# A graph network's layer 0: flags at its end, fewer small vector operations, ranks as whole rows

## The chip, the cores and the metric

The kernel runs on one core of one Trainium2 chip. A core has five engines that run their own instruction streams: TensorE (PE; the loading of its weights is shown apart as PEld), VectorE (DVE), ScalarE (ACT), GpSimd (POOL) and SyncE (SP), which here only issues transfers. Sixteen DMA engines move data between HBM and the core's memory. The metric is the time of one execution on the device in microseconds; a version's time is the median of its runs.

## The reference

Four graph layers work on 2708 nodes with 512 features. Each adds its result to x, and works on h, the normalised and clipped x. The change lies in layer 0, and in the flags that its rows set.

```python
def _L0_gnn_ref(cur, incidence_m):
    mask = incidence_m > 0
    head = mask.astype(...)
    head = head / max(sqrt(sum(head * head, axis=-1)), 1e-12)
    inc = incidence_m + head
    return inc @ cur / sum(inc, axis=-1)
...
h = maximum(_layernorm(x), 0);  x = x + _L0_gnn_ref(h, adj)
h = maximum(_layernorm(x), 0);  x = x + _L1_gnn_ref(h, adj, Wks, Wqs, Wvs, Wo)
h = maximum(_layernorm(x), 0);  x = x + _L2_gnn_ref(h, adj, W1, b1, W3, b3, Wf, bf)
h = maximum(_layernorm(x), 0);  x = x + _L3_gnn_ref(h, adj, W, b)
```

Layer 1 is attention with eight heads, where a score is masked by 1e16 x (1 - adj). With such a factor the softmax of a row is 1 at the row's greatest entry and 0 elsewhere, so the kernel only needs the place of that entry. This holds if no second entry ties with it, if no entry is negative, and if the scores are bounded. The kernel sets a flag where one of these fails, and then runs a general path after the fast one.

## The kernel before, in words

The adjacency is mostly zeros, and its nonzeros lie densest in the first columns and rows. The nodes are cut into NT = 22 tiles of 128 rows (the last has 20). Of a tile m's row of the adjacency, the first DENSE = 6 column tiles are used whole. Of the rest, only the columns that are nonzero somewhere in the tile are fetched, in CHUNKS[m] groups of 128 columns (10 down to 2). The first three tiles use all columns.

Layer 0 is one loop over the tiles (L782), with work for later tiles mixed in:

- *Statistics of a tile* (stats_to, L690). A slab of 128 adjacency rows is loaded (L498). ScalarE takes signs and their sum (L524), clips them and counts (L529), and takes the root of the count (L530). VectorE holds it above 1e-12 (L531) and inverts it (L532): that is rn, the 1/norm. flag_negative (L500) compares the sum of the signs with the count. The row sum is taken (L543) and 1/degree worked out. attended (L549) finds the eight greatest entries of each row (L556) and their places (L558), copies the first place to idx (L559), and scores the first two against each other (L560, L563). Each flag goes into its own column of bad.
- *Lists of columns.* Three tiles form a group. TensorE adds their signs over the rows (count, L265), in four blocks of 485 columns that stand below each other on the partitions. rank_blocks (L316) clips these counts to 0 and 1 (L322) and scans them (L328), so that each column has its rank, and writes the ranks to DRAM (L329) as 128 rows of 485. For each tile load_ranks (L354) reads its four pieces back, spread over all 128 partitions (L362). search (L371) writes an end mark behind the last rank (L378, L379), and finds for each place 1, 2, 3... the first column of that rank (L385). The found column becomes an index for the rows of h (L386), and, in two operations (L395, L403), an index for the adjacency. A last operation (L406) compares the end mark with the capacity of the list.
- *Gathers.* gather_adj (L569) and gather_rows (L588) fetch the listed pieces of the adjacency and rows of h, one indirect transfer from POOL's queue for each 128 places.
- *The incidence* (L626). The 1/norm of a tile's 128 rows is wanted along the free axis, on all partitions. VectorE scales an identity by rn (L631), and TensorE multiplies a matrix of ones with it (L633). Two operations per piece then make mask times 1/norm and add the adjacency (L636, L644), in pieces inc (whole tiles) and incl (listed columns).
- *The product* (L794) adds inc and incl times h in PSUM. Then x is updated (L807), normalised again, and multiplied with the values' weights for layer 1 (after, L727).

What an engine does next is a fixed order. The program is written as above, and a scheduling framework orders each engine's stream when the kernel is built, from its own estimate of what things cost; it also sets the waits between engines. A change in the number of operations can therefore change the order of others. Transfers issued by SP go through one queue in order, and an SP instruction that waits holds back all behind it. Loads of slabs (L498), of dense pieces (L618), of ranks (L362) and of x (L746), and stores of counts (L286), ranks (L329), lists (L659), y (L740) and x1 (L750) all stand in that queue. POOL's queue holds the gathers. Slabs have three buffers, ranks two, gathered pieces three, and gathered rows of h sixteen slots.

After the loop the degrees are added up (L290), and layer 1 gathers rows of y by idx (L1067). The flags are added up in layer 1 and looked at when layer 3 is done (L1371).

Of the kernel before, what the change touches and what calls it, by code (L numbers as in the profile page):

```python
# [9 lines left out]
FP = mybir.dt.float32  # L10
FR = mybir.dt.float32r
BF = mybir.dt.bfloat16
HF = mybir.dt.float16
# [29 lines left out]
def kernel(  # L43
# [89 lines left out]
    rank_b = dram.tile([NGROUP, P, WIDE], HF, name="rank_b")  # L133
    rank_l = dram.tile([1, N], HF, name="rank_l")

    idx = const.tile([P, NT], U32, name="idx")
    BAD_BOUND, BAD_NEG, BAD_MANY = NT, NT + 1, 2 * NT + 1
# [88 lines left out]
    with tc.tile_pool(name="l0_slab", bufs=2) as slabs, tc.tile_pool(  # L226
# [17 lines left out]

        counts = hp.tile([P, GROUP, QUAD], BF, name="counts")
# [70 lines left out]
        def rank_blocks(ms, last_block):  # L316

            rk = hp.tile([P, WIDE], HF, name="rk")  # L320
            sums, offs = (wp.tile([P, 1], FP, name=name) for name in ("sums", "offs"))
            nc.vector.tensor_scalar(  # L322
                rk, last_block, 1.0, None, op0=ALU.min, op1=ALU.add, accum_out=sums
            )
            ahead = ps_list.tile([P, BLK], FP, name="list")
            nc.tensor.matmul(ahead[:, :1], ahead_of, sums, start=True, stop=True)
            nc.scalar.copy(offs, ahead[:, :1])
            nc.vector.tensor_tensor_scan(rk, rk, rk, offs[:, 0:1], ALU.add, ALU.max)  # L328
            nc.sync.dma_start(out=rank_b[ms[0] // GROUP], in_=rk)  # L329

        def rank_rows(ms):

            both = in_slab()
            m = ms[-1]
            r = m % GROUP + 1
            first = dense_of(m) * P
            total = both[QUAD : QUAD + r, :N].bitcast(BF)
            rank = both[:r, :N]
            load_counts(m // GROUP, r, total)
            nc.vector.tensor_scalar_min(rank[:, first:], total[:, first:], 1.0)  # L340
            nc.vector.tensor_tensor_scan(
                rank[:, first:], rank[:, first:], rank[:, first:], 0.0, ALU.add, ALU.max
            )
            if first:
                nc.sync.dma_start(
                    out=rank_b[m // GROUP].rearrange("(b i) w -> i b w", b=4)[:r],
                    in_=rank[:, first:].rearrange("i (b w) -> i b w", b=4),
                )
            else:
                nc.sync.dma_start(out=rank_l, in_=rank)  # L350
# [3 lines left out]
        def load_ranks(m):  # L354
            first = dense_of(m) * P
            num = N - first
            if first:
                ranks = slabs.tile([P, N + 1 - BEHIND], HF, name="ranks", bufs=2)
                q = m % GROUP

                row = rank_b[m // GROUP].rearrange("(b i) w -> i b w", b=4)[q : q + 1]
                nc.sync.dma_start(  # L362
                    out=ranks[:, :num].rearrange("p (b w) -> p b w", b=4),
                    in_=row.to_broadcast([P, 4, WIDE]),
                )
            else:
                ranks = in_slab()[:, : N + 1]
                nc.sync.dma_start(out=ranks[:, :N], in_=rank_l.to_broadcast([P, N]))
            ranks_of[m] = ranks

        def search(m):  # L371
# [5 lines left out]
            end = wp.tile([P, 1], FP, name="end")  # L377
            nc.vector.tensor_scalar_add(end, ranks[:, num - 1 : num], 1.0)  # L378
            nc.vector.tensor_copy(ranks[:, num : num + 1], end)  # L379
            want = wp.tile([P, NCH], FP, name="want")  # L380
            nc.vector.tensor_scalar(want, places, end, None, op0=ALU.min)
            for c0 in range(0, CHUNKS[m], 8):
                c = slice(c0, c0 + 8)
                at = wp.tile([P, 8], U32, name="found")
                nc.vector.max_index(at, want[:, c], ranks)  # L385
                nc.vector.tensor_scalar(  # L386
                    idx_g[:, m, c],
                    at,
                    float(N - first),
                    float(first),  # L390
                    op0=ALU.min,
                    op1=ALU.add,
                )
                node = wp.tile([P, 8], FP, name="node")
                nc.vector.tensor_scalar(  # L395
                    node,
                    at,
                    float(N - 1 - first),
                    float(N // UNIT),
                    op0=ALU.min,  # L400
                    op1=ALU.mult,
                )
                nc.vector.tensor_scalar_add(  # L403
                    idx_a[:, m, c], node, float((first * N + m * P) // UNIT)
                )
            nc.vector.tensor_scalar(  # L406
                bad[:, BAD_MANY + m : BAD_MANY + m + 1],
                end,
                float(CHUNKS[m] * P + 1),
                None,  # L410
                op0=ALU.is_gt,
            )

# [86 lines left out]
        def flag_negative(m, sum_sgn, cnt):  # L500
            n = rows(m)
            nc.vector.tensor_tensor(
                bad[:n, BAD_NEG + m : BAD_NEG + m + 1], sum_sgn[:n], cnt[:n], ALU.not_equal
            )

        def count_signs(m, last):

            sgn = slabs.tile([P, N], BF, name="sgn", bufs=GROUP)
            cnt, sum_sgn = (wp.tile([P, 1], FP, name=name, bufs=4) for name in ("cnt", "sum_sgn"))
            behind(sgn[:1, :1], last)  # L510
            nc.scalar.activation(sgn, slab[m], AF.Sign, accum_out=sum_sgn)
            nc.scalar.activation(sgn, sgn, AF.Relu, accum_out=cnt)
            flag_negative(m, sum_sgn, cnt)

        def row_norm(m):
# [5 lines left out]
            cnt, sum_sgn = (wp.tile([P, 1], FP, name=name, bufs=4) for name in ("cnt", "sum_sgn"))  # L521
# [3 lines left out]
            if m in LATE:  # L525
                cnt = sum_sgn
# [3 lines left out]
            nc.scalar.activation(rn[:n], cnt[:n], AF.Sqrt)  # L530
            nc.vector.tensor_scalar_max(rn[:n], rn[:n], NORM_EPS)  # L531
            nc.vector.reciprocal(rn[:n], rn[:n])  # L532
            if m not in LATE:
                flag_negative(m, sum_sgn, cnt)
# [14 lines left out]
        def attended(m):  # L549
# [5 lines left out]
            top = wp.tile([P, 8], FP, name="top")  # L555
            nc.vector.max(top[:n], ar[:n])  # L556
            at_top = wp.tile([P, 8], U32, name="at_top")
            nc.vector.max_index(at_top[:n], top[:n], ar[:n])  # L558
            nc.vector.tensor_copy(idx[:n, m : m + 1], at_top[:n, 0:1])  # L559
            nc.vector.tensor_scalar(  # L560
                top[:n, 0:2], top[:n, 0:2], 1.0, MASK_SCALE, op0=ALU.subtract, op1=ALU.mult
            )
            nc.vector.tensor_tensor(  # L563
                bad[:n, m : m + 1], top[:n, 1:2], top[:n, 0:1], ALU.is_ge
            )
# [3 lines left out]
        def gather_adj(m):  # L569

            n, num = rows(m), CHUNKS[m]
            for c0 in range(0, num, NCL):
                k = min(NCL, num - c0)
                ac = slabs.tile([P, NCL, P], FP, name="ac", bufs=3)
                for c in range(k):
# [3 lines left out]
                        in_=adj_units,  # L579
                        in_offset=bass.IndirectOffsetOnAxis(  # L580
# [45 lines left out]
        def incidence(m):  # L626
# [3 lines left out]
            dg = wp.tile([P, P], FP, name="dg")  # L630
            nc.vector.tensor_scalar(dg[:n, :n], ident[:n, :n], rn[:n], None, op0=ALU.mult)  # L631
            rb = ps_small.tile([P, P], FP, name="rb")
            nc.tensor.matmul(rb[:, :n], ones[:n], dg[:n, :n], start=True, stop=True)  # L633
# [207 lines left out]
        flush()  # L841
        degrees()
# [3 lines left out]
        flush()  # L846

# [951 lines left out]
```

## Time and profile before

| what | value |
|---|---|
| median of 3 runs | 1415.01 us (1413.84 to 1416.62) |
| profiled execution | 1402.04 us, of which the span is 1400.2 us |
| PE busy | 1278.4 us (91%) |
| DVE busy | 946.6 us (68%) |
| ACT busy | 687.1 us (49%) |
| POOL busy | 662.7 us (47%) |
| mean granted TensorE clock | 0.964 |
| layer 0 | 0 to about 460 us |
| first product of layer 1 (L902) | 477.0 us |

The span reaches from the first to the last instruction of the profiled execution. Busy times are those of instructions that overlap on one engine counted once; a row's mean duration is that of one instruction from its own start to its own end, so the durations of neighbours may overlap. Waits are put down to what came last before the instruction could start. "L531" is a line of the kernel before. Transfers are not counted as work of an engine; the DMA share is how far the sixteen DMA engines were busy.

### The profile page before, as it was taken

The numbers are of one execution on the slowest core, as the hardware profiler recorded it, in microseconds if no ns is written. First come the engines' busy times: TensorE is split into PE (matmuls) and PEld (weight loads), VectorE is DVE, ScalarE is ACT, GpSimd is POOL, SyncE is SP. The second block draws the span as 40 slices with busy tenths as digits, with TensorE's granted clock in tenths as the row PEclk, the third lists the DMA queues.
The fourth block names the chain that finished last, engine by engine and source line by source line (L and its number), as shares of the span: only waits on it lengthen the run. The fifth ranks groups of instructions, "written<-read, shape, count | busy, mean of one in ns | idle before, by whom it ended". The sixth has DMA issues, their size and how long they took to land.

```text
span 1400.2 us, 15615 instructions
## 1 busy us (share of the span) xinstructions
PE 1278.4 (91%) x4478; PEld 768.7 (55%) x4478; DVE 946.6 (68%) x1944; ACT 687.1 (49%) x1051; POOL 662.7 (47%) x673
## 2 busy tenths in 40 slices
PE   4889798998997489899999999899999999978997
PEld 2334344443443357555656666466666666656876
DVE  4778999897997687533434446365666666668686
ACT  5885756742445465422333335244455544556553
POOL 1256677766754411265444441333334344635762
PEclk9999999999998799999999999999999999989999
DMA  9999899999993785487777777756555665858984
GB/s 344 361 306 324 285 379 349 337 331 274 323 323 119 265 295 177 144 269 253 249 214 237 242 222 225 256 166 192 170 165 177 196 203 189 246 160 282 299 262 161
DMA packets 196872, 349.04 MB, mean 249 GB/s; under 512 B 22198, under 2 KB 109840, under 8 KB 193045
## 3 DMA queue, kind: packets, MB, share of 16 engines
q1 hardware_dynamic: 149177, 200.80, 43.0%
q0 software_dynamic: 46032, 145.05, 32.4%
q10 hardware_dynamic: 1568, 2.10, 0.4%
q8 instruction: 37, 0.61, 0.2%
q14 instruction: 58, 0.48, 0.1%
HBM read 284.58 MB, written 63.29 MB: 248 GB/s over the span
## 4 chain that ended last, share of the span: by engine, by line
PE 54%; DMA 5%; DVE 2%; ACT 1%; issue 1%; SPq 0%; POOL 0%; DVEq 0%; ACTq 0%; POOLq 0%
PE aggs L1014 15%; PE main L927 10%; PE agg L1011 8%; PE mixed L927 5%; PE aggs L1011 4%; PE pt L902 3%; PE agg L1202 2%; PE aggs L1202 2%; PE aggs L1026 2%; DMA nz<-nz 1%; DMA wb<-hid 1%; PE pt L1202 1%; PE agg L927 1%; DMA gg<-g1d,idx_g 1%; DMA raw<-in_adj_t_dram 1%
## 5 line engine op out<-in xcount | busy, mean ns | idle before, releaser
L1014 PE MATMUL aggs<-gg,ac 128*128 128x512 f32 (+1 forms) x520 | 233.0, 596 | 3.6 <-DMA gg<-g1d,idx_g 3.6
L962 POOL DMA_INDIRECT gg<-g2d,idx_g x130 | 131.0, 1008 | 218.4 <-PE aggs L1014 170.2
L962 POOL DMA_INDIRECT gg<-g1d,idx_g x130 | 133.6, 1027 | 173.4 <-PE aggs L1014 103.3
L576 POOL DMA_INDIRECT ac<-in_adj_t_dram,idx_a x130 | 133.6, 1028 | 89.3 <-issue 31.3
L794 PE MATMUL acc<-h,inc 128*128 128x512 f32 (+1 forms) x348 | 163.2, 617 | 12.8 <-DVE inc L644 12.6
L1014 PEld LDWEIGHTS aggs<-gg,ac 128*128 128x128 f32 (+1 forms) x520 | 97.9, 189 | 110.7 <-issue 102.4
L594 POOL DMA_INDIRECT h<-h0d,idx_g x111 | 113.3, 1021 | 33.8 <-issue 21.3
L998 ACT ACTIVATE a_hi<-raw 128x384 fp32r<-128x384 f32 x84 | 43.6, 520 | 160.7 <-issue 87.2
L1011 PE MATMUL agg<-ghi,a_hi 128*128 128x512 f32 x252 | 114.9, 456 | 3.3 <-ACT a_hi L998 3.1
L794 PEld LDWEIGHTS acc<-h,inc 128*128 128x128 f32 (+1 forms) x348 | 65.4, 196 | 91.6 <-issue 74.0
L1011 PE MATMUL agg<-glo,a_lo 128*128 128x512 f32 x252 | 102.1, 405 | 3.2 <-ACT glo L207 3.2
L794 PE MATMUL acc<-h,incl 128*128 128x512 f32 (+1 forms) x222 | 103.3, 611 | 0.0
L1011 PE MATMUL aggs<-gs,a_s 128*128 128x512 f32 x252 | 100.5, 402 | 0.6 <-DVE gs L204 0.6
L999 DVE TENSOR_TENSOR a_lo<-raw,a_hi 128x384 fp32r<-128x384 f32 x84 | 47.2, 562 | 73.5 <-ACT a_hi L998 45.2
L158 PE MATMUL yacc<-wvo,hT 128*128 128x512 f32 (+1 forms) x176 | 85.6, 627 | 3.2 <-ACT hT L193 3.2
L908 DVE SCALAR_TENSOR_TENSOR v_lo<-pt,v_hi 128x512 fp32r<-128x512 f32 (+1 forms) x88 | 56.4, 664 | 44.6 <-ACT v_hi L907 44.1
L962 POOL DMA_INDIRECT gg<-hidr,idx_h x62 | 64.8, 1046 | 42.7 <-PE aggs L1202 16.4
L889 DVE SCALAR_TENSOR_TENSOR u<-aggs,u 128x512 f32<-128x512 f32 x42 | 28.8, 686 | 76.6 <-PE aggs L1014 75.1
L907 ACT ACTIVATE v_hi<-pt 128x512 fp32r<-128x512 f32 (+1 forms) x88 | 48.4, 578 | 45.0 <-PE pt L902 43.1
L794 PEld LDWEIGHTS acc<-h,incl 128*128 128x128 f32 (+1 forms) x222 | 42.5, 196 | 50.4 <-issue 47.8
L524 ACT ACTIVATE sgn<-ar 128x2708 bf16<-128x2708 f32 (+1 forms) x22 | 54.0, 2455 | 27.1 <-DMA ar<-in_adj_dram 26.6
L556 DVE MAX8 top<-ar 128x8 f32<-128x2708 f32 (+1 forms) x22 | 65.3, 2969 | 0.0
(321 smaller groups left out, 2788.9 us busy)
## 6 DMA issues: line engine op xcount, KB each, us to landing
ar<-in_adj_dram SPq DMA_DIRECT2D x27, 1354.0 KB
raw<-in_adj_t_dram SPq DMA_DIRECT2D x122, 192.0 KB
slot<-x SPq DMA_DIRECT2D x41, 256.0 KB
at<-in_adj_t_dram SPq DMA_DIRECT2D x27, 384.0 KB
ranks<-rank_b SPq DMA_DIRECT2D x20, 485.0 KB
ac<-lst SPq DMA_DIRECT2D x16, 384.0 KB
h<-in_x_dram SPq DMA_DIRECT2D x21, 256.0 KB
h0d<-h POOLq DMA_DIRECT2D x21, 256.0 KB, 7.2
```

The source lines that it names most:

```text
L158: nc.tensor.matmul(acc[:n], hT[:, c, :n], w[:, c, :], start=(c == 0), stop=(c == NCD - 1))
L524: nc.scalar.activation(sgn[:n], ar[:n], AF.Sign, accum_out=sum_sgn[:n])
L556: nc.vector.max(top[:n], ar[:n])
L576: nc.gpsimd.indirect_dma_start(out=ac[:, c, :n], out_offset=None, in_=adj_units, in_offset=bass.IndirectOffsetOnAxis(ap=idx_a[:, m, c0 + c ...
L594: nc.gpsimd.indirect_dma_start(out=g, out_offset=None, in_=h0d[:, :], in_offset=bass.IndirectOffsetOnAxis(ap=idx_g[:, m, c : c + 1], axis=0),)
L794: product = nc.tensor.matmul(acc[:n], a, g, start=(i == 0), stop=(i == len(pairs) - 1))
L908: nc.vector.scalar_tensor_tensor(lo[d], pt[d], 0.0, hi[d].bitcast(FP), op0=ALU.max, op1=ALU.subtract)
L927: nc.tensor.matmul(acc[:n], a[:, c, :n], b[:, c, :], start=first and c == 0, stop=last and c == NCD - 1,)
L962: nc.gpsimd.indirect_dma_start(out=gs[c], out_offset=None, in_=gd[:, :], in_offset=bass.IndirectOffsetOnAxis(ap=index[:, m, c : c + 1], ax ...
L1011: nc.tensor.matmul(acc[:n], a[:k, i, :n], b[:k], start=st, stop=sp)
L1014: nc.tensor.matmul(mixed[:n], a, g, start=(c == 0 and not dense_of(m)), stop=(c == len(chunks) - 1),)
L1202: nc.tensor.matmul(bank_h(m)[: rows(m)], a, b, start=(i == 1), stop=(i == total))
```

## The change

Five things change, all in layer 0.

- The greatest entries (tops, at_top), the counts and sign sums (cnts, sums_sgn) and the end marks (ends) of all tiles are kept in tiles with one column per row tile. A new function flags() works all flags out from these, once, after the loop. Flags move to other columns of bad. idx is copied once for all tiles.
- The lower bound of the norm goes into the root as a bias of 1e-24, so the maximum falls away. Its place in the order is ScalarE's L539, then the inverse.
- 1/norm is spread by one product of rn, read 128 times along the free axis, with the identity. The scaled identity is gone.
- A search makes the adjacency's index in one operation. The constant part of the address is given to the indirect transfer as an offset.
- Ranks are stored with their end mark as whole rows of 1941 elements. rank_blocks adds 1 behind the last rank and writes its four blocks with four transfers; rank_rows adds it likewise. load_ranks reads one contiguous row, spread over the partitions, and search only copies the end mark.

```diff
-    rank_b = dram.tile([NGROUP, P, WIDE], HF, name="rank_b")
-    rank_l = dram.tile([1, N], HF, name="rank_l")
+    rank_b = dram.tile([NGROUP, GROUP, 4 * WIDE + 1], HF, name="rank_b")
+    rank_l = dram.tile([1, N + 1], HF, name="rank_l")
...
+        for t, v in ((cnts, 0.0), (sums_sgn, 0.0), (ends, 0.0), (tiny, NORM_EPS * NORM_EPS)):
+            nc.gpsimd.memset(t, v)
+        for t in range(NT):
+            nc.gpsimd.memset(caps[:, t : t + 1], float(CHUNKS[t] * P + 1))
...
+        def flags():
+
+            score = wp.tile([P, NT, 2], FP, name="score", bufs=1)
+            nc.vector.tensor_scalar(
+                score, tops[:, :, 0:2], 1.0, MASK_SCALE, op0=ALU.subtract, op1=ALU.mult
+            )
+            nc.vector.tensor_tensor(bad[:, :NT], score[:, :, 1], score[:, :, 0], ALU.is_ge)
+            nc.vector.tensor_tensor(
+                bad[:, BAD_NEG : BAD_NEG + NT], sums_sgn, cnts, ALU.not_equal
+            )
+            nc.vector.tensor_tensor(bad[:, BAD_MANY : BAD_MANY + NT], ends, caps, ALU.is_gt)
...
-            nc.sync.dma_start(out=rank_b[ms[0] // GROUP], in_=rk)
+            nc.vector.tensor_scalar_add(end, row_end[:, wide - 1 : wide], 1.0)
+            for b in range(4):
+                w = wide + b // 3
+                nc.sync.dma_start(
+                    out=rank_b[ms[0] // GROUP, : len(ms), b * wide : b * wide + w],
+                    in_=row_end[b * QUAD : b * QUAD + len(ms), :w],
+                )
...
-                nc.sync.dma_start(
-                    out=ranks[:, :num].rearrange("p (b w) -> p b w", b=4),
-                    in_=row.to_broadcast([P, 4, WIDE]),
-                )
+                row = rank_b[m // GROUP, q : q + 1, : num + 1]
...
+            nc.sync.dma_start(out=ranks, in_=row.to_broadcast([P, num + 1]))
...
-            end = wp.tile([P, 1], FP, name="end")
-            nc.vector.tensor_scalar_add(end, ranks[:, num - 1 : num], 1.0)
-            nc.vector.tensor_copy(ranks[:, num : num + 1], end)
+            end = ends[:, m : m + 1]
+            nc.vector.tensor_copy(end, ranks[:, num : num + 1])
...
-                node = wp.tile([P, 8], FP, name="node")
                 nc.vector.tensor_scalar(
-                    node,
+                    idx_a[:, m, c],
                     at,
                     float(N - 1 - first),
                     float(N // UNIT),
                     op0=ALU.min,
                     op1=ALU.mult,
                 )
-                nc.vector.tensor_scalar_add(
-                    idx_a[:, m, c], node, float((first * N + m * P) // UNIT)
-                )
-            nc.vector.tensor_scalar(
-                bad[:, BAD_MANY + m : BAD_MANY + m + 1],
-                end,
-                float(CHUNKS[m] * P + 1),
-                None,
-                op0=ALU.is_gt,
-            )
...
-            nc.scalar.activation(rn[:n], cnt[:n], AF.Sqrt)
-            nc.vector.tensor_scalar_max(rn[:n], rn[:n], NORM_EPS)
+            nc.scalar.activation(rn[:n], cnt[:n], AF.Sqrt, bias=tiny[:n])
             nc.vector.reciprocal(rn[:n], rn[:n])
-            if m not in LATE:
-                flag_negative(m, sum_sgn, cnt)
...
-            nc.vector.tensor_copy(idx[:n, m : m + 1], at_top[:n, 0:1])
-            nc.vector.tensor_scalar(
-                top[:n, 0:2], top[:n, 0:2], 1.0, MASK_SCALE, op0=ALU.subtract, op1=ALU.mult
-            )
-            nc.vector.tensor_tensor(
-                bad[:n, m : m + 1], top[:n, 1:2], top[:n, 0:1], ALU.is_ge
-            )
...
+                        element_offset=dense_of(m) * P * N + m * P,
...
-            dg = wp.tile([P, P], FP, name="dg")
-            nc.vector.tensor_scalar(dg[:n, :n], ident[:n, :n], rn[:n], None, op0=ALU.mult)
             rb = ps_small.tile([P, P], FP, name="rb")
-            nc.tensor.matmul(rb[:, :n], ones[:n], dg[:n, :n], start=True, stop=True)
+            nc.tensor.matmul(
+                rb[:, :n], rn[:n].to_broadcast([n, P]), ident[:n, :n], start=True, stop=True
+            )
...
         flush()
+        nc.vector.tensor_copy(idx, at_top[:, :, 0])
         degrees()
...
         flush()
+        flags()
```

## The prediction

> **What bounds the kernel now.** The page comes first: which engines are busy in the slices that layer 0 fills (a slice is 35 us, so the first 13).
>
> ```profile
> PE   4889798998997489899999999899999999978997
> DVE  4778999897997687533434446365666666668686
> POOL 1256677766754411265444441333334344635762
> DMA  9999899999993785487777777756555665858984
> ```
>
> PE, DVE and the DMA engines all stand at 8 or 9. So I cut out the stretch in which the vector engine has no rest, from 80 us (the first list is searched) to 452 us (the last row maximum), and the part of it in which the gathers run densest:
>
> ```profile
> 80.00:452.00 372.00, 336.38 (x913) 151.11 (x912) 346.09 (x723) 206.38 (x251) 248.47 (x244) 0.96 0.90 304
> 80.00:290.00 210.00, 193.58 (x542) 87.03 (x541) 196.27 (x428) 137.67 (x161) 147.16 (x150) 0.97 0.94 325
> ```
>
> The columns are length, then busy us (and instructions) of PE, PEld, DVE, ACT, POOL, then clock, DMA share, GB/s. Of 372 us DVE works 346, PE 336. What is left is told by the waits of the first 500 us:
>
> ```profile
> DVE end L378 <- DMA ranks<-rank_b: 21.0, 6, 6.3
> PE acc L794 <- DVE inc L644: 12.6, 7, 3.4
> PE rb L633 <- DVE dg L631: 9.6, 6, 3.7
> PE rb L633 <- DVE deg L544: 3.8, 1, 3.8
> ```
>
> DVE hardly waits for anything but rank lists; PE's idle time ends at DVE. DVE is therefore the engine that sets the pace, PE is 10 us of work behind it, and a stall of DVE goes straight to PE. One such place, from the timelines of DVE and PE:
>
> ```profile
> 224.88 0.15 DVE L378 TENSOR_SCALAR end<-ranks 128x1 f32<-128x1 f16 x1 [3.26 <-DMA ranks<-rank_b]
> 224.95 0.17 DVE L178 BATCH_NORM_AGGREGATE mv<-stats 128x2 f32<-128x6 f32 x1
> 225.04 0.12 DVE L531 TENSOR_SCALAR rn<-rn 128x1 f32<-128x1 f32 x1
> 225.08 0.15 DVE L379 CAST ranks<-end 128x1 f16<-128x1 f32 x1
> ...
> 228.62 0.27 DVE L631 TENSOR_SCALAR dg<-ident,rn 128x128 f32<-128x128 f32 x1
> 228.80 2.98 DVE L556 MAX8 top<-ar 128x8 f32<-128x2708 f32 x1
> ```
> ```profile
> 220.02 5.32 PE L794 MATMUL acc<-h,inc 128*128 128x512 f32 x12
> 229.03 0.77 PE L633 MATMUL rb<-dg,ones 128*128 128x128 f32 x2 [3.69 <-DVE dg L631]
> 229.59 7.69 PE L794 MATMUL acc<-h,incl 128*128 128x512 f32 x12
> ```
>
> A late rank list (3.26 us) makes the scaled identity late, and PE stands still for 3.69. After it twelve rows take 7.69 us where twelve took 5.32 before: the granted clock was 0.88 and 0.78 in the slices 220 to 240. A gap of PE so costs about 2.4 us more than its length.
>
> **The change, part by part.**
>
> *DVE instructions taken away.* Six kinds go once per row tile, 22 each: the max on the norm (L531), the scaled identity (L631), the copy of the index (L559), the score and its comparison (L560, L563), the sign comparison (L502): 132. Of a search go the bound flag (L406) and one of the two that make the end mark (L378, L379), 21 each, and of 23 groups of places one of two (L395, L403). That is 132 + 42 + 23 = 197.
>
> What one costs is the choice that matters most. The rows give 0.12 to 0.17 us for most (L531 126 ns, L559 142, L395 160 in the middle case) and 0.27 for L631. But instructions overlap: above, starts follow each other after 70, 90, 40 and 60 ns. Taking for each removed instruction the distance to DVE's next start, at most its own length, over the whole trace, I get 1.2 us for L531, 4.6 for L631, 1.5 for L559, 1.5 for L560, 1.7 for L563, 1.4 for L502, 1.7 for L406, 1.3 for the end mark, 1.6 for L395: 16.4 us in sum. The Trainium skill (VectorE: DVE Perf Modes, section on the errata of operations with SBUF sources) speaks for more: a fixed term measured as about 150 cycles at 0.96 GHz, 0.156 us, exposed between instructions; by it 197 would be 31 us. The starts in the trace decide: 16.4, and 31 is the far end.
>
> *DVE instructions added.* Eight adds for the end mark, five operations for the flags and the index, 13 in all. At 0.08 us (the distances above) 1.0 us; the five of 22 to 44 columns are near L304 (0.29 us), but in the build's order all but one stand near the end, where DVE waits 8.5 us for the degrees (L304 on PE). Cover gone, they cost 1 us. A small part (six of L531, a few of L631) lies before 80 us, where DVE is not the bound. Left: 16.4 - 1.0 = 15.4, of which I count **14 us** on the path.
>
> *Rank lists as whole rows.* A load was 512 packets of 970 B; now 128 of 3882 B. In the trace's packet records the middle 970 B packet took 45 ns, the middle 4096 B packet 159 ns (25.8 B/ns). 512 x 45 / 16 engines = 1.44 us against 128 x 151 / 16 = 1.20: 0.24 us, or 5 us of engine time over 20 loads. The Trainium skill (DMA: Bandwidth & Descriptors, Specifications) sets line rate at 512 B and above, so by it the gain is nothing; the packets say 0.24, and since 0.90 of the DMA time is taken, both are small. What counts is the wait. The load issued at 219.40 let DVE go at 224.88, 5.5 us, most of it queue and sharing. I give each of the six waits 0.5 us (bounds: 0 to 1.5).
>
> *Rank rows written in four pieces.* L329 was one SP issue of 0.35 us per group; four are 1.4, so the ranks are asked for 1.0 us later, plus one small DVE add. Before each load SP now waits for four landings instead of one (SP stood 19.4 us in six such waits). Behind it on SP queue the next slab (L498), the list (L659) and the store of x; slabs are prefetched, their waits end on ACT (26.6 us), which has slack in this stretch (206 of 372). Against this, the build's order moves the first search of two groups (rows 9 to 11 and 12 to 14) behind a whole row maximum of the next tile, two instructions of 2.97 us: their waits (1.0 and 3.3 us) go. The six waits, 6.3, 3.8, 1.0, 3.3, 2.9, 3.8, become by +1.0 - 0.5 each, and less the moved work, about 4, 4, 0, 0, 4, 4: 16 instead of 21. **5 us** gained; ends 12 and -4.
>
> *1/norm spread directly.* rb is now one product of the same shape with rn as weights, so PE's time stays; a weight read with step 0 is not in the trace: bounds 0 and one more load of 0.15 us, 22 times, 3 us; I take 0, by the row of the same shape. L631 has been counted.
>
> *Indices in one operation.* The constant part goes into the gather's offset. The gathers are the same 241 POOL instructions of 0.94 us that start 1.25 us apart (bounds: 0 to 0.1 us each; I take 0, since nothing in the descriptor's form changes).
>
> *Memsets.* 29 more on POOL near 2 to 5 us, 0.09 us each, 2.6 us. POOL was idle until 25.26; without that cover they would cost their 2.6.
>
> *What comes back.* Two limits are close behind DVE. In 80 to 290 us POOL has 150 instructions 1.25 us apart, 187 of 210 us, so that stretch can't lose more than 22. The DMA engines carry 0.94 of it. PE's floor: 336 less the half-clock stretches. If DVE loses 19, it is at 346 - 14 = 332 beside PE's 336: two engines level, with buffers of two or three, wait for each other more. I take back 4 of the 19 (ends 0 and 12); the removed gaps' slow clock (2.4 us for each of the nine PE gaps over 1.9 us in this stretch, 22 at most) stands against it and is in the upper end.
>
> **Sum:** -14 - 5 + 4 = **-15 us**, in the stretch 80 to 452 alone. The profiled execution (1402.04 us, of which 1400.2 is span and 1.8 lies around it) would come to 1387. The median of the runs, 1415.01, lies 13 us above that execution, for a cause the profile does not show; I take the difference over: 1415 - 15 = **1400**.
>
> **Rivals.**
>
> *The others hold the line.* POOL's chain of gathers, or the transfers, are the bound where DVE seems to be, and the freed DVE time turns into waits. For it: POOL at 187 of 210 us, DMA at 0.94. Against it: PE's idle time ended at DVE, hardly ever at a gather. Gain 0 to 5: 1412.
>
> *More than the sum.* Each short PE gap that goes takes its half-clock time with it, and small instructions cost their full 0.15 us. 31 - 1 + 5 + some clock = 35 at most: 1383.
>
> *Slower: the rank rows come too late.* The four pieces go through SP one after the other, and in the build's order a slab load that waits for DVE stands between the third and the fourth piece of rows 12 to 14; list and x stores stand between the pieces and the loads of two more groups. If a group's ranks come more than 3 us later than now (14 + 5 = 19 us over six groups), the gain is eaten; at 5 us later, 30 - 19: 1426. For it: SP's queue is in order and already waits 88.7 us for x stores at L746. Against it: the new place of the search gives two groups 6 us more, and the issue itself adds 1.0.
>
> *No effect of the parts at all* (the small work was hidden) has against it that DVE is in one piece from 80 to 452; it goes with the first rival.
>
> **How the numbers follow.** Likeliest, gain 8 to 28 (1387 to 1407): 0.65. Others hold the line: 0.15, half of it within 0.2% (2.8 us, about what a measurement here can tell from no change). More than the sum: 0.11. Slower: 0.09. So faster 0.65 + 0.11 + 0.07 = 0.83, same 0.08, slower 0.09. The range leaves out the slower case and the far end of the great gain: 1384 to 1414.
>
> **What would show it.** Right: between 80 us and the last row maximum DVE's instructions fall from 723 to about 550 and its busy time by more than 25 us (lengths, not distances); the stretch is some 15 us shorter; PE's waits for the scaled identity are gone; after layer 0 nothing moves. Wrong: rank waits above 25 us, PE waiting for gathers (incl on DMA), or the same length of layer 0 with DVE idle.

## The result and the profile after

Over 20 runs each, the changed kernel took 1401.68 us (median; 1394.82 to 1412.15) and the kernel before 1410.72 us (1399.44 to 1419.34). The ratio is 0.9938, with a 95% interval of 0.9915 to 0.9961: 8.7 us less, 5.5 to 12.0. The forecast was 1400 us, 15 us less. The forecast time is nearer than the forecast gain, because more runs moved the kernel before from 1415.01 down to 1410.72. Ratios here and below compare fast runs alone: two runs of e6, and one of the kernel before beside e9 to e12, were over 1.5% above the fastest of their kernel and are left out.

The profiled execution of the changed kernel took 1403.91 us (span 1402.0). That of the kernel before, 1402.04 us, had been one of its quickest. So the two profiles show where work and waits lie, but not the gain itself.

The rows of the page that were shown of before, now of the changed kernel:

```profile
PE   4889989979988489999999999899999999978997
DVE  4787989886997588623434446365566656658786
POOL 2255677776555311165444441333334344634762
DMA  9999899998993975487777777856555666748984
```

DVE has lost a tenth in several slices of layer 0. PE has not gained there. The same two stretches as before (length, then busy us and instructions of PE, PEld, DVE, ACT, POOL, then clock, DMA share, GB/s):

```profile
80.00:452.00 372.00, 331.68 (x907) 149.93 (x906) 329.47 (x543) 205.80 (x248) 244.20 (x241) 0.95 0.89 301
80.00:290.00 210.00, 193.67 (x542) 87.67 (x541) 185.30 (x310) 136.21 (x156) 145.87 (x148) 0.95 0.94 321
```

DVE went from 723 to 543 instructions and from 346.09 to 329.47 us of work: 16.6 us less. But PE did no more work in the same 372 us (336.38 before, 331.68 now). Taken from 60 us to the last product of layer 0's sum (439.8 us before, 441.2 now), DVE's rest rose from 34.2 to 47.7 us and PE's from 33.3 to 36.9. In these two executions the freed time of DVE has almost all become rest of DVE. The waits of the first 500 us tell where the rest is (total us, times, longest):

```profile
DVE ends L407 <- DMA ranks<-rank_b: 26.5, 9, 7.9
...
PE rb L629 <- DVE incl L634: 13.1, 3, 7.0
...
PE list L355 <- DVE rk L351: 11.0, 3, 8.9
PE acc L792 <- DVE inc L642: 10.7, 6, 4.8
```

The waits for rank lists are 26.5 us, not the forecast 16. PE no longer waits for a scaled identity, but for two other things of DVE: the incidence (L634), which still reads the spread norm of the tile before (rb has one buffer), and the clipped counts of a group (L351, 11.0 us; the same wait was 0.3 us before).

How these hang together, from DVE's and PE's timelines of the changed kernel, where tiles 9 to 11 are searched:

```profile
184.40 0.15 DVE L407 CAST ends<-ranks 128x1 f32<-128x1 f16 x1 [6.08 <-DMA ranks<-rank_b]
184.49 0.95 DVE L634 SCALAR_TENSOR_TENSOR inc<-at,rb 128x768 f32<-128x768 f32 x1
...
188.53 1.07 DVE L634 SCALAR_TENSOR_TENSOR incl<-ac,rb 128x896 f32<-128x896 f32 x1
```
```profile
189.74 0.77 PE L629 MATMUL rb<-ident,rn 128*128 128x128 f32 x2 [5.72 <-DVE incl L634]
190.30 7.22 PE L792 MATMUL acc<-h,inc 128*128 128x512 f32 x12
```

DVE stands 6.08 us for a rank list. Behind it wait the two incidence operations that free rb. PE then stands 5.72 us, and its next twelve products take 7.22 us (granted clock 0.73 from 190.3 to 197.5 us), where twelve took 5.32 before (clock 1.00 from 220.0 to 225.3). As I read this, fewer instructions ahead of L407 would only have let DVE arrive there earlier.

Why that list is late, from DVE's and SP's timelines of the changed kernel:

```profile
163.38 1.22 DVE L357 TENSOR_TENSOR_SCAN rk<-rk,offs 128x485 f16<-128x485 f16 x1
...
164.56 2.98 DVE L562 FIND_INDEX8 at_top<-tops,ar 128x8 uint32<-128x2708 f32 x1
167.45 0.14 DVE L358 TENSOR_SCALAR rk<-rk 128x1 f16<-128x1 f16 x1
```
```profile
167.55 0.88 SPq L361 DMA_DIRECT2D rank_b<-rk  x3
168.53 0.36 SPq L514 DMA_DIRECT2D ar<-in_adj_dram  x1
168.99 0.24 SPq L361 DMA_DIRECT2D rank_b<-rk  x1
171.78 0.34 SPq L657 DMA_DIRECT2D lst<-ac  x1
172.18 0.42 SPq L738 DMA_DIRECT2D y<-yo  x1
177.63 0.80 SPq L397 DMA_DIRECT2D ranks<-rank_b  x2
```

The scan ends at 164.6. The small end mark (L358) stands behind the 2.98 us in which a row maximum's place is found, so the pieces go out at 167.55. A slab load stands between the third and the fourth. The ranks are read only at 177.63, 13.0 us after the scan; before it was 4.9. Most of this passes between the end of the fourth piece's issue and the read (8.4 us); for the last 4.9 us SP does nothing but wait for that piece to land.

### The profile page after: what moved, and what is told of

Same layout as the page of the kernel before. It is cut to its first block, busy times and chain, and to the rows that moved or that the text cites. A ratio compares the mean times of both kernels' runs of the same rounds, so it can differ in the third digit from the quotient of the medians.

```text
span 1402.0 us, 15500 instructions
## 1 busy us (share of the span) xinstructions
PE 1274.1 (91%) x4478; PEld 768.7 (55%) x4478; DVE 931.4 (66%) x1760; ACT 689.0 (49%) x1051; POOL 655.7 (47%) x702
## 5 line engine op out<-in xcount | busy, mean ns | idle before, releaser
L792 PE MATMUL acc<-h,inc 128*128 128x512 f32 (+1 forms) x348 | 168.0, 631 | 10.7 <-DVE inc L642 10.7
L158 PE MATMUL yacc<-wvo,hT 128*128 128x512 f32 (+1 forms) x176 | 82.4, 611 | 1.0 <-ACT hT L193 1.0
L962 POOL DMA_INDIRECT gg<-hidr,idx_h x62 | 63.6, 1026 | 41.8 <-PE aggs L1202 15.7
L180 ACT ACTIVATE rstd<-mv,eps 128x1 f32<-128x1 f32 x88 | 24.5, 289 | 83.2 <-DVE mv L178 61.1
L562 DVE FIND_INDEX8 at_top<-tops,ar 128x8 uint32<-128x2708 f32 (+1 forms) x22 | 65.3, 2970 | 0.0
```

What stands on the lines that cost most here:

```text
L158: nc.tensor.matmul(acc[:n], hT[:, c, :n], w[:, c, :], start=(c == 0), stop=(c == NCD - 1))
L562: nc.vector.max_index(at_top[:n, m, :], tops[:n, m, :], ar[:n])
L792: product = nc.tensor.matmul(acc[:n], a, g, start=(i == 0), stop=(i == len(pairs) - 1))
L962: nc.gpsimd.indirect_dma_start(out=gs[c], out_offset=None, in_=gd[:, :], in_offset=bass.IndirectOffsetOnAxis(ap=index[:, m, c : c + 1], ax ...
```

## The experiments

My first theory (theory 1 in the expectations) was that the DVE savings are worth about 15 us and the four-piece rank write gives some of it back. The rival (theory 2) was that the freed DVE time turns into waits. "The planner" is the scheduling framework that orders each engine's stream. Ratios are to the kernel before on the same chip. The runs were made on different chips: e5 to e8 together on one where the kernel before took 1482 us, all others on chips where it took 1408 to 1411. Only ratios are compared between them.

| kernel | ratio | 95% interval | runs |
|---|---|---|---|
| changed kernel | 0.9938 | 0.9915 to 0.9961 | 20 |
| e1 rank part undone | 0.9970 | 0.9952 to 0.9989 | 22 |
| e2 rank part alone | 0.9920 | 0.9893 to 0.9947 | 6 |
| e3 one write, whole rows | 0.9983 | 0.9967 to 1.0000 | 22 |
| e4 174 small operations added | 0.9972 | 0.9957 to 0.9987 | 22 |
| e5 order at the end (1482 us chip) | 0.9872 | 0.9823 to 0.9920 | 6 |
| e6 before, order at the end (same) | 0.9993 | 0.9968 to 1.0018 | 20 |
| e7 one write, search later (same) | 0.9916 | 0.9884 to 0.9948 | 10 |
| e8 changed kernel again (same) | 0.9953 | 0.9926 to 0.9979 | 19 |
| e9 direct spread alone | 1.0001 | 0.9984 to 1.0019 | 22 |
| e10 small work alone | 1.0006 | 0.9987 to 1.0025 | 14 |
| e11 e5 again | 0.9929 | 0.9911 to 0.9948 | 22 |
| e12 e7 with the order at the end | 0.9977 | 0.9958 to 0.9996 | 22 |

The table's ratios are those on record. Where runs are few, the plain ratio of the medians differs from them: e2 0.9933, e5 0.9905, e7 0.9936, e10 0.9990.

**e1: the rank part undone.** The core of the edit to the changed kernel:

```diff
-            nc.vector.tensor_scalar_add(end, row_end[:, wide - 1 : wide], 1.0)
-            for b in range(4):
-                w = wide + b // 3
-                nc.sync.dma_start(
-                    out=rank_b[ms[0] // GROUP, : len(ms), b * wide : b * wide + w],
-                    in_=row_end[b * QUAD : b * QUAD + len(ms), :w],
-                )
+            nc.sync.dma_start(out=rank_b[ms[0] // GROUP], in_=rk)
...
-            nc.sync.dma_start(out=ranks, in_=row.to_broadcast([P, num + 1]))
+                nc.sync.dma_start(
+                    out=ranks[:, :num].rearrange("p (b w) -> p b w", b=4),
+                    in_=row.to_broadcast([P, 4, WIDE]),
+                )
...
-            nc.vector.tensor_copy(end, ranks[:, num : num + 1])
+            nc.vector.tensor_scalar_add(end, ranks[:, num - 1 : num], 1.0)
+            nc.vector.tensor_copy(ranks[:, num : num + 1], end)
```

> The changed kernel with its rank part undone: rank rows written in one transfer and read block by block as before, the end mark made in each search by two operations; all other parts kept. Theory 1 (the removed DVE work is worth about 15 us and the four-piece write gives some 7 of it back through later rank lists): about 1395 us, 0.989 of the kernel before, waits for rank lists between 80 and 452 us back from 26 to 15 to 21 us. Theory 2 (the other engines and the transfers hold the line; lists come late to a DVE that is merely early): the same as the changed kernel, about 1402 us or 0.994, with the waits moved to other places.

It took 0.997. My first theory falls: undoing the supposed loss did not add to the gain, it took about half away. DVE did as little work between 80 and 452 us as in the changed kernel (329.87 us), yet the kernel gains only 4.2 us over before. Where the freed time went shows in DVE's waits for rank lists over the whole execution, here of e1, e9, e10 and e4 in this order:

```profile
DVE ends L405 <- DMA ranks<-rank_b: 28.9, 6, 9.6
DVE end L378 <- DMA ranks<-rank_b: 28.5, 6, 7.1
DVE ends L405 <- DMA ranks<-rank_b: 30.3, 6, 9.2
DVE ends L414 <- DMA ranks<-rank_b: 18.1, 4, 7.7
```

The first three write the ranks as the kernel before does, and have 10.5 to 16.2 us less DVE work from 80 to 452 us; their waits are 7.5 to 9.3 us longer than its 21.0. e3 and e12 show the same (29.3 and 29.6). The trip from the scan to the search, which DVE itself starts with its scan, takes 13.1 us in e1 and took 11.7 before: work removed between the two does not shorten it.

**e2: the rank part alone**, put into the kernel before (the edit of e1 the other way round).

> The kernel before with the rank part alone: four pieces written, whole rows read, the end mark made once where the ranks are made. Theory 1: slower than before by 3 to 8 us (ratio 1.002 to 1.006), waits for rank lists up by 4 us or more. Theory 2: no slower, ratio 0.997 to 1.001. The prediction's own step (5 us gained) would give 0.996.

0.992: the part that I had taken for the loss is, alone, worth 11 us (7 to 15), more than the whole change at its middle. Only six runs stand behind it, but all lie below 1401. Their mean granted clock was also higher (0.967, against 0.963 for the kernel before beside them); whether that is a cause or an effect is not told. The parts do not add: 4.2 and 11 us alone, 8.7 together. The waits for rank lists fell from 21.0 to 19.0 us, too little for 11 us. In the profile layer 1 starts 6.1 us earlier (470.9 for 477.0), and 4.8 us of that lie after the last product of layer 0's sum, where no rank list is read. So what this run gained by is not shown.

What the part does change shows against kernels that have the rest of the change alike. One write stores all 128 partitions of a group, of which twelve hold ranks that are read; the four store those twelve alone (the issues of before, then of the changed kernel, KB each):

```profile
rank_b<-rk SPq DMA_DIRECT2D x6, 121.2 KB
...
rank_b<-rk SPq DMA_DIRECT2D x18, 2.8 KB
rank_b<-rk SPq DMA_DIRECT2D x6, 2.8 KB
```

SP waits for this write to land before it asks for the lists: 19.4 us in all before and 10.1 in e2, and with less DVE work 27.6 to 33.5 us with one write (e1, e3, e9, e10, e12) and 17.6 to 21.1 with four (changed kernel, e4, e11). DVE's waits for the lists go the same way (28.5 to 30.3 us with one, 18.1 to 26.5 with four). These are single profiles; the changed kernel and e11, which do the same work up to the end of layer 0, differ by 6.7 us in DVE's waits.

**e3: one write, into whole rows.** As the changed kernel, but the rank rows go out in one transfer and the end mark is made in the search.

```diff
-            for b in range(4):
-                w = wide + b // 3
-                nc.sync.dma_start(
-                    out=rank_b[ms[0] // GROUP, : len(ms), b * wide : b * wide + w],
-                    in_=row_end[b * QUAD : b * QUAD + len(ms), :w],
-                )
+            nc.sync.dma_start(
+                out=rank_b[ms[0] // GROUP].rearrange("i (b w) -> b i w", b=4), in_=rk
+            )
...
-                row = rank_b[m // GROUP, q : q + 1, : num + 1]
+                row = rank_b[m // GROUP, q : q + 1]
```

> The changed kernel with the rank rows written by one transfer into whole rows (no end column; the end mark is made in the search by two operations), and whole rows read. It parts the reading from the four writes. Theory 1: the four writes and the late end mark are the loss, so about 1394 us, 0.988 of before, a little better than with block reads. If the whole-row reading itself is the loss: no better than the changed kernel, 0.994. Theory 2: 0.994 as well, with short waits for rank lists.

0.9983, level with e1. Reading whole rows is therefore not what the rank part gains by. What is left of it: the four transfers and the smaller amount that they write, the end mark made with the ranks, and the order that the planner makes of them.

**e4: small work added.** The changed kernel with 174 operations on one element per row.

```diff
+        def extra(m, src, n, *ks):
+            for k in ks:
+                nc.vector.tensor_scalar_add(spare[:n, m, k : k + 1], src, 1.0)
...
+            extra(m, tops[:n, m, 0:1], n, 0, 1, 2)
...
+            extra(m, rn[:n], n, 3, 4, 5)
...
+            extra(m, end, P, 6, 7)
```

> The changed kernel with about 174 small DVE operations added (one element per row, results not used): three after each row norm, three after each row maximum, two in each search. It prices one small DVE operation on the path. By the distances between starts (0.08 to 0.09 us each) +15 us: 1416 us, ratio 1.004. By their length in the records (0.12 us) +21 us: ratio 1.009. By the fixed term of 0.156 us +27 us: ratio 1.013. Theory 2 (DVE is not what holds the line): +0 to 4 us, ratio 0.994 to 0.997.

0.9972 against 0.9938: 0.0034, or 4.8 us (1 to 9, the two intervals taken together), that is 0.03 us for each. In the profiles 3.1 us of the loss lie at the end of layer 0 (from the last product of its sum to layer 1's first: 43.1 us, 40.0 in the changed kernel), so in the loop the price may be lower still. Its row for 80 to 452 us:

```profile
80.00:452.00 372.00, 331.51 (x909) 149.39 (x907) 338.50 (x691) 207.03 (x250) 244.23 (x237) 0.96 0.89 300
```

DVE has 148 instructions and 9.0 us more than the changed kernel there (0.06 us each), and PE does the same work in the stretch (331.51 against 331.68). So even the time that a small operation adds to DVE's busy total is only half on the path; its own length (0.14 us in the groups of this run) is not near it. DVE's waits for rank lists are 8.4 us shorter than in the changed kernel (18.1 for 26.5), near the 9.0 us added; but e11 shows how far one profile can be off there (19.8).

**e9: the direct spread alone**, in the kernel before:

```diff
-            dg = wp.tile([P, P], FP, name="dg")
-            nc.vector.tensor_scalar(dg[:n, :n], ident[:n, :n], rn[:n], None, op0=ALU.mult)
             rb = ps_small.tile([P, P], FP, name="rb")
-            nc.tensor.matmul(rb[:, :n], ones[:n], dg[:n, :n], start=True, stop=True)
+            nc.tensor.matmul(
+                rb[:, :n], rn[:n].to_broadcast([n, P]), ident[:n, :n], start=True, stop=True
+            )
```

> The kernel before with the direct spread of 1/norm alone (the scaled identity and its DVE operation gone). From the runs so far, the seam (last product of layer 0's sum to first product of layer 1) and the stretch before it are told apart: the seam is 37.3 us in the kernel before, and with this kernel's order at the end expected near 33 (-4). If the scaled identity is what the removed DVE work is worth (its PE waits go, 12 us in the profile of before), the stretch gives 6 to 9 us more: ratio 0.991 to 0.993. If it is worth only its distances to the next start (4.6 us): 0.994. If nothing: 0.997.

1.0001: not even the 0.997 that I had expected if the removed work were worth nothing. The end of layer 0 came to 34.0 us, 3.3 shorter, as foreseen, and the time still did not move. Either the rest lost as much, or the time does not follow the length of the end in one profile; which, is not shown. So 22 operations of 0.3 us and the waits of PE for them are worth nothing that can be seen. Its row, and PE's waits at the spread:

```profile
80.00:452.00 372.00, 336.44 (x902) 152.01 (x902) 334.92 (x694) 201.77 (x245) 244.56 (x235) 0.94 0.89 301
```
```profile
PE rb L631 <- DVE incl L636: 11.7, 4, 5.4
PE rb L631 <- DVE top L560: 5.0, 1, 5.0
```

DVE does 11 us less than before in the stretch (in part because this execution had come less far: its last product ended at 448.1 us), and PE the same work. PE's waits at this product between 60 and 460 us were 17.3 us in four rows before (9.6, 3.8, 3.5, 0.4), and are 16.7 in these two. The scaled identity was the last of several things that this product waits for. With it gone, the next one ends the wait.

**e10: the small work alone**: e1 with the scaled identity put back (the edit of e9 the other way round).

> The changed kernel with the rank part undone and the scaled identity put back: only the flags, the index copy, the norm's maximum and the second operations of the indices are gone (about 140 small DVE operations). By the prediction's distances (11 us) less a longer seam (+3): ratio 0.994. If a small operation is worth what adding them cost (174 for about 5 us with the seam): 1.000 (0.998 to 1.001), the longer seam eating the gain.

1.0006: nothing, as the price from e4 and a longer end foretold (from the last product of layer 0's sum to the first of layer 1 42.2 us, where the kernel before took 37.3). e1, which has both parts, bounds the whole DVE part of the change, beside the old rank write, at 1.5 to 6.8 us.

**e5, e6, e11: the order at the end of layer 0.** In the profiles I also found the stretch from the last product of layer 0's sum to layer 1's first product longer: 40.0 us (441.2 to 481.2) in the changed kernel, 37.3 (439.8 to 477.0) before. PE's timeline of the changed kernel there:

```profile
449.65 0.70 PE L192 MATMUL pt<-ident,hn 128*128 128x128 f32 x4 [4.81 <-ACT hn L186]
451.04 3.78 PE L158 MATMUL yacc<-wvo,hT 128*128 128x512 f32 x4 [0.69 <-ACT hT L193]
454.75 0.32 PE L324 MATMUL list<-ones_b,ar 27*128 27x1 bf16 x6
...
457.87 0.62 PE L324 MATMUL list<-ones_b,ar 27*128 27x1 bf16 x16
...
481.22 1.97 PE L902 MATMUL pt<-ident,slot 128*128 128x128 f32 x8 [18.45 <-ACT slot L186]
```

The products for the degrees (L324) stand among the last tiles' values, which layer 1 waits for, and on DVE the last row maximum stood ahead of the last norms (4.81 us of wait at 449.65). In e5 the order was set by hand:

```diff
-        degrees()
+        with tc.issue_after(normed_last):
+            attended(LATE[-1])
+        nc.vector.tensor_copy(idx, at_top[:, :, 0])
         after(NT - 2, None)
         after(NT - 1, hns.pop(NT - 1))
-        after(NT - 1, None)
+        last = after(NT - 1, None)
         flush()
+        with tc.issue_after(last):
+            degrees()
```

> The changed kernel with the order at its end set by hand: the last row maximum stands behind the norm of the last tile on DVE, the products for the degrees behind the last tile's values on PE. No work is added or taken away. Theory 3 (the change's new order at the end of layer 0 takes back part of its gain: from the last row maximum to the first product of layer 1 the changed kernel takes 32.5 us where the kernel before took 29.2): that stretch 22 to 25 us, and 8 us off the time: ratio 0.988. If layer 1's first gathers wait for something else (its weights or bias): the first product moves by less than 2 us, ratio 0.993 to 0.995.

> The kernel before with the same order set at the end of layer 0, nothing else. By theory 3 its stretch of 29.2 us comes to 22 to 25 us: 4 to 7 us off, ratio 0.995 to 0.997. With the run of the changed kernel with this order it tells what the change is worth when both have the same end of layer 0: by theory 3 their ratio is about 0.992 (11 us); if the removed work is worth nothing, 1.000.

> The changed kernel with the order at its end set by hand, again: only 6 runs stood behind 0.987. Seam 38.8 us against 40 to 42: expected ratio 0.987 to 0.992, and 3 us below the changed kernel.

The stretch came to 38.8 us (e5 and e11 alike), not to 22 to 25: I had first measured it from the last row maximum, which the edit itself moves later. In the kernel before it is 37.0 with the edit (e6, on the 1482 us chip) and 37.3 without (on the other), and the time the same (0.9993, where 0.995 to 0.997 had been expected). For the changed kernel e5 gives 0.9872 against 0.9953 of e8 beside it, e11 0.9929 against 0.9938, just outside the 0.987 to 0.992 expected. Both point the same way. The gap is outside chance only on the one chip, with six runs. With the same end of layer 0, e5 stands to e6 as 0.988 to 1 (0.992 foreseen). The step is settled as far as this: the new order lengthened the end of layer 0 by 2.7 us, and an order set by hand takes 1.2 of it back (3.0 on the other chip, where e8 had 41.8). e11 took 1397.59 us, below both kernels (1408.25 for the kernel before beside it); that it is quicker than the changed kernel is likely, and not shown beyond doubt.

**e7, e12: the place of a search.** e3 with the first search of tiles 9 to 11 behind the row maximum of tile 12, as in the changed kernel; e12 has the order at the end as well.

```diff
-                do_next()
+                if t != 4 * GROUP:
+                    do_next()
...
-                    attended(t)
+                    found = attended(t)
+                if t == 4 * GROUP:
+                    with tc.issue_after(found):
+                        do_next()
```

> The kernel with one write into whole rows, and the first search of rows 9 to 11 moved behind the row maximum of row 12 as the changed kernel's order has it. It parts the order from the four transfers. If the place of the search is what the rank part gains by: ratio 0.994, and 4 us off the wait of this search at about 175 us (5.05 us). If it is the four transfers or the end mark made with the ranks: 0.998 as without the move.

> The kernel with one write into whole rows, the search of rows 9 to 11 moved behind the row maximum of row 12, and the end's order set by hand. If both gains add (0.9916 for the first two, 3 us for the order at the end): ratio 0.989, level with or just below the changed kernel with its end set by hand; seam 38 to 39 us.

e7 gave 0.9916, which spoke for the search's place. But e12, with the same place and the order at the end (37.0 us), gave 0.9977, level with e3, where 0.989 had been expected. The wait at this search, 5.05 us in e3, is gone in e12, but the waits for rank lists are as long in all (29.6 us for 29.3): they have moved to other searches. The two disagree, and were run on different chips. I take from them only that the place of this one search does not carry the gain on the chip that e12 ran on. There e11, which differs from e12 in the rank write, the end mark and what the planner makes of them, took 7.3 us less (1397.59 against 1404.89, 22 runs each). In their profiles that gain lies ahead of the end of layer 0: the last product of the sum ends at 436.2 us in e11 and at 443.8 in e12.

**e8: the changed kernel again.**

> The changed kernel again, unchanged, beside the others and for a second profile. Expected 0.994 (0.992 to 0.996). In the profile: the last row maximum at 446 to 450 us and the first product of layer 1 some 32 us later, waits for rank lists 22 to 28 us; if the two places differ by more than 3 us from the first profile, the places of a single profile can't carry differences of that size.

0.9953, in agreement. As a second profile it did not serve: on this chip the last product of the sum came at 494.0 us, not 441.2. The waits for rank lists were 6.7 us, not the 22 to 28 expected. With nearly the same ratio, these waits can't be the whole account there; what holds the line on that chip is open.

## Why the prediction was right or wrong

**Right, by the size of the sum, and in part by chance.** The gain is 8.7 us, not 15; the time was inside the range. Step by step:

- *DVE instructions taken away and added:* right as an amount of work. 15.4 us were forecast over the whole kernel and 15.2 measured (946.6 to 931.4 us of DVE work); in the stretch it was 16.6 (346.09 to 329.47), not the "more than 25" named as a sign of being right. The choice of the starts (16.4) over the fixed term of the Trainium skill (VectorE: DVE Perf Modes, the section on errata; 31 us by it) was right on DVE's side.
- *"Of which I count 14 us on the path":* this is the step that failed. The small work alone gave 1.0006, the spread alone 1.0001, both together 0.997: 4.2 us (1.5 to 6.8). On top of the rank part the DVE part shows no gain at all (0.9938 with it, 0.9920 without, in e2's six runs). Adding small operations cost 0.03 us each, not 0.08. I had read an engine that works 346 of 372 us as the one that sets the pace, and a wait that ends at DVE as one that DVE's work causes. But DVE itself stands at rank lists, and much of what it saves ahead of them becomes wait: its rest up to the last product of the sum rose by 13.5 us, and in the kernels with less DVE work and the old write the waits for rank lists alone rose from 21.0 to 28.5 to 30.3 us. Two of the prediction's own signs of being wrong came: rank waits above 25 us (26.5), and layer 0 as long as before with DVE idle (441.2 us to the last product, 439.8 before).
- *What comes back, 4 us:* mis-sized for the same reason. Of the 15.4 us, about 11 came back. The rival "the others hold the line" described the DVE part rightly (0 to 5 us). It was wrong for the change as a whole, since the rank part gains. Which of the others holds the line (PE, the transfers, or the chain through SP's queue) no run here tells.
- *1/norm spread directly:* PE's time did stay. L631's 4.6 us were worth nothing alone, and PE's waits moved on (17.3 us at the product before, 16.7 in e9, 13.1 in the changed kernel, with 11.0 new ones at L355).
- *Rank rows:* the forecast of 5 us has the right sign and size (0.992 alone; 0.9938 against 0.997 on top of the rest, 4.5 us), but by luck. Its own terms do not give it: with +1.0 - 0.5 us each, the four waits that stay come to about 19 us in place of 16, so 2 us gained and not 5; and work moved away ahead of a wait makes it longer. The waits were to fall to 16 us and rose to 26.5: the removed DVE work lengthened them (28.9 in e1), and the rank part took a little off again. The search's new place gave nothing in e12. Whole-row reads gave nothing (e3): the packets took what was foretold (3882 B in 152 ns in the middle case, 151 forecast), but the 0.24 us for each load was worth nothing that these runs can see, as the rule of the Trainium skill (DMA: Bandwidth & Descriptors, Specifications) had it, against the packet rows. The four landings had been counted as a cost; with the rest alike, SP stood 21.1 us for them and 30.8 for the one (e1). What the gain is, is open: the four transfers come with a tenth of the bytes, with the end mark and with another order of DVE's and SP's instructions, and no run parts these. One transfer of the twelve rows alone, and four with the old order, were not tried.
- *The slower rival:* its mechanism is there. The slab does stand between the third and the fourth piece, of tiles 9 to 11 (not 12 to 14), and the ranks were read 13.0 us after the scan instead of 4.9. But the lateness is not the pieces' doing: on the mean of the six groups the lists were read 7.8 us after the scan (6.0 before), and 7.8 with one write too (e1). By the rival's sum 3 us later would have eaten the gain; the search came 3.1 us later (14.8 us after the scan for 11.7), and the gain stood.
- *The order at the end, costed at nothing:* the five operations were hidden, as said. But the order around them changed and the end of layer 0 became 2.7 us longer. I had looked at what the added work covers, not at what the planner moves for it.
- *Sums:* the nine terms given as 16.4 us add up to 16.5, and a gain of 35 us leads to 1380, not 1383. Neither moves the forecast.

## What to carry to other kernels

A high busy share does not make an engine the one that sets the pace. Look at what its own waits end at: where it stands at a transfer that it has itself started, work removed between the start and that point mostly turns into longer waiting (here 16 us less work was worth 4.2 us). Price small work by adding some: 174 dummy operations told more than any row of durations. Where a planner orders the instructions, compare the whole order, the stage's end included, because an edit's side effect there can be as large as the edit.

## What the runs showed of the hardware that was not expected

- A small DVE operation of 0.14 us by its record added 0.06 us to DVE's busy time (148 instructions, 9.0 us) and 0.03 us to the kernel.
- The same kernel took 1408 us on some chips and 1482 on another. In the changed kernel's two profiles, layer 0's last product came 53 us later there (494.0 against 441.2) and the rest took 26 us longer (946.6 against 920.8 us, from layer 1's first product on). Between 80 and 452 us its DMA share was 0.84, not 0.89, and its granted clock 0.90, not 0.95. The cause is open.
- From run to run of one kernel, a shorter time mostly went with a higher mean granted clock (correlation -0.67, -0.58 and -0.78 over the three sets of runs of the kernel before, -0.85 in e1, -0.21 in e4). Which causes which is not shown.
